# Routing in ten even pieces, four softmax rows on VectorE from step 48, and the shared expert of two groups inside attention's last steps

## The chip, the cores and the metric

The kernel runs on one core of a Trainium2 chip. Its time is the device time of one execution in microseconds (us). PE is TensorE (matrix products; PEld its weight loads), DVE is VectorE, ACT is ScalarE, POOL is GpSimd, SP is SyncE, which issues most transfers (DMA). Each engine works through its own list of instructions in order; one that waits for a semaphore holds back everything behind it on that engine.

## What is computed

The input is 4096 tokens (16 sequences of 256) of 128 numbers, in float32. Two layers follow each other; in each, `x = x + attention(norm(x)) + ffn(norm(x))`. The change touches layer 0 alone:

```python
xn = layernorm(x)
# attention: 8 heads of 64, windows of 128 (a block of 256 queries sees 256 keys under a mask)
qkv = (layernorm(xn) * ln_g + ln_b) @ w_qkv.T       # q and k rotated by position
out = softmax(mask(q @ k.T)) @ v @ w_out.T
# ffn: 8 routed experts, two for each token, and one shared expert
probs = softmax(xn @ router_w + router_b); two largest -> weights
shared = gelu(xn @ sw1 + sb1) @ sw2 + sb2
routed = sum over the two experts of weight * (gelu(xn @ rw1[e] + rb1[e]) @ rw2[e] + rb2[e])
x = x + out + shared + routed
```

Layer 1 (a gated attention unit and 32 experts) comes after it and has the same code in both kernels but for one helper that is called in other pieces.

## The kernel before

**Tiling.** Tokens go in 8 groups of 512 (`G`), a group being 4 chunks of 128 tokens, and two sequences. Layer 0's attention is a loop of 64 steps (line 531, s from -3 to 64): one step is one sequence and one pair of heads, eight steps are a group (`g, r = divmod(s, 8)`). The loop is software-pipelined and its order is written by hand: inside `tc.manual_schedule` (line 497) every engine gets its instructions in the order of the program text. What one turn of the loop at step s issues, in this order:

- copies left from the turn before (`later`): on ACT, the values `v` out of PSUM (line 363) and `here`, a copy of the q/k projection (387), whose halves four DMAs on SP exchange into `there`;
- on PE, the 8 transposes of the weights of step s (`turned0`, 456); on ACT, their eviction to `pT` (463), and then the 4 exponentials of step s+2 (433), each with its row sum;
- on DVE, every second step `near` (q and k times cosine, 394, two of 512 columns);
- on DVE, `divided` for step s+1 (439 to 442): a reciprocal and **three of the four** row blocks times it. The fourth is done by ACT (`divided_last`, 447), later in the same turn, behind the exponentials;
- on DVE, on the other steps, `far` ("there" times sine, 398);
- `scores` for step s+3: 4 matmuls on PE (417; the profile counts each fp32 matmul twice) and 4 reductions on DVE (423) that add the mask, move the scores out of PSUM and take the row maximum;
- `sums` (402): cosine part plus sine part, on POOL for pairs of heads 1 to 23 (`FREE = 24`, line 370), on DVE for 0 and 24 to 31;
- then one piece of the routing, of the preparing or of the placing, if the tables of due times say so (below);
- ACT's fourth row block (447); on PE the product with the values of step s-1 (`attended`, 473), on ACT its copy (478);
- on odd steps the next q/k projection (`rotated`, 377), on r = 0 and 2 a half of the output projection (`project`, 486), on r = 4 and 6 two of the four value projections (362).

**Side work in the loop.** For each group `routed` (334) makes norms, transposes the normalised tokens, and calls `route0` (214): router matmuls (219), logits and maximum (222 to 225), exponential (228), and then in one piece sum, reciprocal, probabilities and `before` (197), which ranks the 8 probabilities of a token by 8x8 comparisons in five operations (203 to 212). The dictionary `pieces` (512) gives group g = 1 to 7 a first step of -6, -1, 4, 10, 15, 21, 26 and its pieces 0, 2, 5, 6, 7, 8 and 9 steps later. `prepare` (349) makes the second normalisation, and its first piece (`xh`, 173) is due at r = 6, two groups ahead. `places0` (239) counts tokens for each expert in eight pieces, from step 37; its results `slot_at` and `tile_off` say in which row of `x_rows` (in HBM) a token goes. From step 43 each turn issues three scatters on POOL (316, 64 in all), each behind one ACT instruction of the same turn.

**After the loop** (686) the shared expert of groups 0 and 1 (`shared0`, 608: two matmuls with `sw1`, two Gelus, two matmuls with `sw2`, an add into `yTs`) and the routed experts (706): 39 tiles of 256 rows, each fetched (643 weights, 645 rows) by SP, transposed, multiplied, and stored. Here a scheduler orders the instructions. The buffers of this stage lie where attention's were, so that the first fetch waits for the last use of them. The other six groups' shared expert is done in layer 1's beginning (934 to 940).

PSUM has 8 banks: two for scores (`s`), two for transposes (`t`), one for `o`, three for all else (`mm`); `turn` (61, 602) says from which tags `mm_tile` takes its banks.

Of the kernel before, what the change touches and what calls it, by code (L numbers as in the profile page):

```python
# [47 lines left out]
def two_layers(ctx: ExitStack, tc: tile.TileContext, a: dict, out: bass.AP):  # L48
# [17 lines left out]
    def mm_tile(name):  # L66
        tags, n = turn
        turn[1] += 1
        return bank(tags[n % len(tags)], name)
# [125 lines left out]
        return d  # L195

    def before(rank, v, tie, n, name):

        v_o = v.unsqueeze(2).to_broadcast([P, NC, n, n])
        v_i = v.unsqueeze(3).to_broadcast([P, NC, n, n])  # L200
        gt = small.tile([P, NC, n, n], F32, tag=f"gt{n}", name=f"gt_{name}", bufs=2)
        eq = small.tile([P, NC, n, n], F32, tag=f"eq{n}", name=f"eq_{name}", bufs=2)
        nc.vector.tensor_tensor(gt, v_o, v_i, ALU.is_gt)
        nc.vector.tensor_tensor(eq, v_o, v_i, ALU.is_equal)
        nc.vector.tensor_tensor(
            eq.rearrange("p c i j -> p c (i j)"),
            eq.rearrange("p c i j -> p c (i j)"),
            tie.unsqueeze(1).to_broadcast([P, NC, n * n]),
            ALU.mult,
        )  # L210
        nc.vector.tensor_tensor(gt, gt, eq, ALU.add)
        nc.vector.tensor_reduce(rank, gt, AX.X, ALU.add)

    def route0(g, xnT):

        ps_r = mm_tile(f"rt_{g}")
        ps_r = ps_r[:, : NC * E0].rearrange("p (c e) -> p c e", e=E0)
        for c in range(NC):
            nc.tensor.matmul(ps_r[:, c, :], xnT[:, c * P : (c + 1) * P], rtw, start=True, stop=True)
        yield  # L220
        lg = small.tile([P, NC, E0], F32, tag="lg", name=f"lg_{g}")
        nc.vector.tensor_tensor(lg, ps_r, rtb, ALU.add)
        mx = small.tile([P, NC], F32, tag="rmx", name=f"rmx_{g}")
        nc.vector.tensor_reduce(mx, lg, AX.X, ALU.max)
        nc.vector.tensor_tensor(lg, lg, mx.unsqueeze(2).to_broadcast([P, NC, E0]), ALU.subtract)
        yield
        pr = pr_all[:, g * NC : (g + 1) * NC, :]
        nc.scalar.activation(pr, lg, AF.Exp)
        yield
        sm = small.tile([P, NC], F32, tag="rsm", name=f"rsm_{g}")  # L230
        nc.vector.tensor_reduce(sm, pr, AX.X, ALU.add)
        nc.vector.reciprocal(sm, sm)
        nc.vector.tensor_tensor(pr, pr, sm.unsqueeze(2).to_broadcast([P, NC, E0]), ALU.mult)
        before(rk_all[:, g * NC : (g + 1) * NC, :], pr, tie0, E0, f"r0_{g}")
        yield

    scattered = []
# [75 lines left out]
    def scatter0(n, behind):  # L313
# [12 lines left out]
        )  # L326
        scattered.append(ins)


    yTs, xnTs = [], []  # L330
    with first as pa:
        wk = pa.enter_context(tc.tile_pool(name="wkA", bufs=2))

        def routed(g):
            xn = xn_all[:, g * NC : (g + 1) * NC, :]
            stats = moments(xs[g], f"a{g}")
            yield
            again(r2_all[:, g, :], *normalise(xn, xs[g], *stats), f"b{g}")
            yield
            t = transposed(xn, f"xnT_{g}")  # L340
            xnT = keep.tile([P, G], F32, tag="xnT", name=f"xnTs_{g}")
            nc.scalar.copy(xnT, t)
            xnTs.append(xnT)
            yield
            yield from route0(g, xnT)
# [21 lines left out]

        paces = [None] * 3
        later, turning = [], []
        FREE = 24  # L370

        def rotated(n):

# [63 lines left out]

        def divided(s, pr, sm):
            nc.vector.reciprocal(sm, sm)
            for n in range(3):  # L440
                row = pr[:, n // 2, n % 2, :]
                nc.vector.tensor_scalar(row, row, sm[:, n : n + 1], None, ALU.mult)  # L442

# [53 lines left out]
        with tc.manual_schedule(engines={order.PE, order.DVE, order.Activation, order.Pool}):  # L497
# [11 lines left out]
                fs.clear()  # L509


            pieces = {}
            for g, begin in zip(range(1, NG), (-6, -1, 4, 10, 15, 21, 26)):
                for d in (0, 2, 5, 6, 7, 8, 9, 10):
                    pieces.setdefault(begin + d, []).append(g)

            step(routing, 0, 2)
            step(preparing, 0, 2)
            rotated(0)
            drain(later)  # L520
# [1 line left out]
            near, far, sums = turning.pop(0)  # L522
            near()
            step(routing, 0)
            step(routing, 1, 2)
            far()
            sums()
            drain(later)
# [2 lines left out]
            for s in range(-3, NS + 1):  # L531
                g, r = divmod(s, 8)
                if 0 <= s < NS:
                    tps = turned0(s, sc.pop(s)[0])
                drain(later)
                if 0 <= s < NS:
                    pTs[s] = evicted(s, tps)
                if 0 <= s + 2 < NS:
                    sms[s + 2] = exponentials(s + 2, *sc[s + 2])
                if turning and len(turning[0]) == 3:  # L540
                    turning[0].pop(0)()
                    far = sums = None
                else:
                    far, sums = turning.pop(0) if turning else (None, None)
                if 0 <= s + 1 < NS:
                    sm = sms.pop(s + 1)
                    divided(s + 1, sc[s + 1][0], sm)
                if far:
                    far()
                if s + 3 < NS:  # L550
                    sc[s + 3] = scores(s + 3)
                if sums:
                    sums()

                if s in (-3, -2, -1, 5):
                    step(routing, 0)
                if s == -2:
                    step(preparing, 1)
                for n in pieces.get(s, ()):
                    step(routing, n)  # L560
                if r == 0:
                    step(preparing, g + 1)
                if s >= 0 and r == 6:
                    step(preparing, g + 2)
                if s == 37:
                    placing = places0(wk)
                if 37 <= s < 45:
                    next(placing)
                if 0 <= s + 1 < NS:
                    divided_last(sc[s + 1][0], sm)  # L570
                if s >= 1:
                    attended(s - 1, pTs.pop(s - 1))

                if s % 2 and 2 <= (s + 7) // 2 < NS // 2:
                    rotated((s + 7) // 2)
                if s < -1:
                    for c in range(2):
                        values(0, 2 * (s + 3) + c)
                if s < 0:
                    continue  # L580
                if 0 < g < NG and r in (0, 2):
                    project(g - 1, r // 2)
                if s == NS - 2:
                    project(NG - 1, 0)
                if r in (4, 6) and g + 1 < NG:
                    values(g + 1, r - 4)
                    values(g + 1, r - 3)
                if s == 2:
                    zero = w_a.tile([P, 2 * D], F32, tag="zero", name="zero")
                    nc.gpsimd.memset(zero, 0.0)  # L590
                    x_r0 = x_rows.rearrange("(t p c) d -> p t (c d)", p=P, c=2)

                if s >= 2 and s % 2 == 0 and s - 2 < NT0:
                    n = min(2, NT0 - (s - 2))
                    nc.sync.dma_start(
                        out=x_r0[:, s - 2 : s - 2 + n, :], in_=zero.unsqueeze(1).to_broadcast([P, n, 2 * D])
                    )
                if s >= 43:
                    for n in range(3 * (s - 43), min(3 * (s - 42), 2 * NG * NC)):
                        scatter0(n, paces[n % 3])  # L600
            project(NG - 1, 1)
    turn[0] = ["mm", "s", "mm", "o", "mm", "s"]


    late = ctx.enter_context(tc.tile_pool(name="late", bufs=1))
    spread = ctx.enter_context(tc.tile_pool(name="spread", bufs=4))

    def shared0(g, wk):
        hs = []
        for c in range(2):  # L610
            hp = mm_tile(f"hs_{g}_{c}")
            nc.tensor.matmul(hp, sw1[:, c * P : (c + 1) * P], xnTs[g], start=True, stop=True)  # L612
            h = wk.tile([P, G], F32, tag="h1", name=f"hss_{g}_{c}", bufs=6)
            nc.scalar.activation(h, hp, AF.Gelu, bias=col("sb1", c))
            hs.append(h)
        yield
        yp = acc_tile(f"y1_{g}")
        for c, h in enumerate(hs):
            nc.tensor.matmul(yp, sw2[:, c, :], h, start=(c == 0), stop=(c == 1))
        nc.vector.tensor_tensor(yTs[g], yTs[g], yp, ALU.add)  # L620
        yield

    with ExitStack() as pb:
        wk = pb.enter_context(tc.tile_pool(name="wkB", bufs=2))
# [58 lines left out]
            nc.vector.tensor_tensor(y, yp, bias, ALU.add)  # L683
            nc.sync.dma_start(out=yr[t], in_=y)

        for g in range(2):
            for _ in shared0(g, wk):
                pass
        stage = [fetched, turned, hidden, down]
        at = [0, 4, 5, 6]  # L690
        state = {}
# [31 lines left out]
    with ExitStack() as pc:  # L723
# [207 lines left out]
        begun = {n: pair(0, n) for n in range(-1, 3)}  # L931
        with tc.manual_schedule(engines={order.PE, order.DVE, order.Activation, order.Pool}):

            shared = {f"y{g}": shared0(g, wk) for g in range(2, NG)}
            steps1 = {"n": finish0(0), "r": choice, "a": attention, "f": coming,
                      **{f"p{n}": b for n, b in begun.items()}, **shared}
            for what in (
# [136 lines left out]
```

## Time and profile before

| what | us |
| --- | --- |
| median of 3 runs | 962.4 |
| lowest, highest | 961.96, 965.62 |
| the profiled execution itself | 969.97 |
| its span, from which all times below are counted | 968.2 |
| first exponential of step 0 starts | 33.83 |
| of step 48; of step 58; last exponential of the loop ends | 277.25; 329.53; 358.8 |
| last matmul of attention ends, first fetch of the routed experts is issued | 372.0; 372.12 |
| PE, DVE, ACT, POOL busy, of the span | 94%, 73%, 51%, 30% |

How to read it: busy shares over the whole span mix stages with different limits, so the views used below are cut at the times in the table. A profile line of a group has its source line, engine, operation, tiles and count, then busy time, mean duration in ns of one, and the idle time just before them with the engine and line that ended it. The chain of waits is followed back from the last instruction, each step to what released it. The granted clock is the share of PE's full clock in a stretch.

### The profile page before, as it was taken

How to read it: one execution, taken by the hardware profiler on the slowest of the kernel's cores; microseconds unless marked ns; L12 is line 12 of the kernel's file. 1: busy time of each engine (PE TensorE's matmuls, PEld its weight loads, DVE VectorE, ACT ScalarE, POOL GpSimd, SP SyncE). 2: the span in 40 equal slices, each digit the busy share in tenths (PEclk: the TensorE clock that was granted, in tenths of full speed). 3: DMA queues.
4: the chain of work that ended last, by engine and by line, in shares of the span. 5: the costliest groups of instructions: out<-in, count | busy, mean ns of one | idle time of the engine just before them, and what ended most of it. 6: DMA issues, size and time to landing. Idle time of an engine off the chain costs nothing.

```text
span 968.2 us, 13569 instructions
## 1 busy us (share of the span) xinstructions
PE 909.4 (94%) x3848; PEld 516.2 (53%) x3848; DVE 705.3 (73%) x2247; ACT 498.6 (51%) x1216; POOL 286.1 (30%) x253
## 2 busy tenths in 40 slices
PE   2998999999999888998989999999999999999997
PEld 1555566565555444988445445454455545455453
DVE  4699999889999741333379588686876868778663
ACT  1688889889787873433352233433324342243411
POOL 2242343332355562000353124241242512321200
PEclk8799999999999999999999999999999999999999
DMA  6061111011122115787135432323333243321430
GB/s 194 23 218 45 28 24 33 24 27 29 28 69 64 58 39 188 223 256 222 42 77 131 103 77 70 99 76 98 77 97 91 63 93 96 92 77 44 101 87 11
DMA packets 64921, 84.54 MB, mean 87 GB/s; under 512 B 10320, under 2 KB 40784, under 8 KB 64336
## 3 DMA queue, kind: packets, MB, share of 16 engines
q1 hardware_dynamic: 60320, 74.75, 28.8%
q0 software_dynamic: 4096, 8.40, 2.8%
q8 instruction: 31, 0.51, 0.2%
q10 hardware_dynamic: 432, 0.53, 0.2%
q14 instruction: 42, 0.34, 0.1%
HBM read 58.22 MB, written 17.04 MB: 78 GB/s over the span
## 4 chain that ended last, share of the span: by engine, by line
PE 59%; DVE 23%; issue 6%; DMA 5%; ACT 3%; POOL 2%; SPq 2%; DVEq 0%; ACTq 0%; POOLq 0%
PE u L919 9%; PE g L917 7%; PE z L954 7%; PE s L417 5%; PE o L473 3%; DVE p L423 3%; PE y L486 3%; PE t L456 3%; PE h L665 3%; PE yr L676 3%; DVE p L442 2%; DMA y_rows<-yt 2%; PE z L972 2%; PE o L892 1%; PE pq L377 1%
## 5 line engine op out<-in xcount | busy, mean ns | idle before, releaser
L921 ACT ACTIVATE h<-g 128x512 f32<-128x512 f32 x128 | 75.2, 594 | 234.5 <-PE g L917 222.3
L923 DVE TENSOR_TENSOR h<-h,u 128x512 f32<-128x512 f32 x128 | 87.3, 683 | 63.8 <-PE u L919 57.0
L917 PE MATMUL g<-xn1Ts,eg 128*128 128x512 f32 x256 | 131.4, 595 | 0.0
L919 PE MATMUL u<-xn1Ts,eu 128*128 128x512 f32 x256 | 131.2, 597 | 0.0
L433 ACT ACTIVATE p<-p,nm 128x256 f32<-128x256 f32 x256 | 127.6, 515 | 0.3
L954 PE MATMUL z<-h,ed 128*128 128x512 f32 x224 | 114.2, 593 | 0.0
L423 DVE CUSTOM_DVE_ANT_0 p<-s,mask 128x256 f32<-128x256 f32 x256 | 92.9, 419 | 16.0 <-PE s L417 15.2
L732 POOL DMA_INDIRECT yg<-y_rows,slot_at x64 | 69.7, 1090 | 114.4 <-PE hs L612 96.1
L417 PE MATMUL s<-k,q 64*128 64x256 f32 x512 | 85.2, 420 | 12.2 <-DVE k L402 7.6
L926 DVE TENSOR_TENSOR h<-h,bc 128x512 f32<-128x512 f32 x128 | 90.3, 708 | 2.7
L456 PEld LDWEIGHTS t<-ident,p 128*128 128x128 f32 x512 | 59.1, 140 | 51.1 <-ACT p L447 13.2
L456 PE MATMUL t<-ident,p 128*128 128x128 f32 x512 | 69.4, 275 | 14.0 <-ACT p L447 9.0
L316 POOL DMA_INDIRECT x_rows<-xn_all,slot_at x64 | 63.7, 996 | 52.0 <-ACT pT L463 15.2
L463 ACT COPY pT<-t 128x512 f32<-128x512 f32 x128 | 69.5, 598 | 18.4 <-PE t L456 13.9
L919 PEld LDWEIGHTS u<-xn1Ts,eu 128*128 128x128 f32 x256 | 48.1, 193 | 54.4 <-issue 47.8
L954 PEld LDWEIGHTS z<-h,ed 128*128 128x128 f32 x224 | 42.5, 190 | 53.3 <-issue 46.5
L917 PEld LDWEIGHTS g<-xn1Ts,eg 128*128 128x128 f32 x256 | 46.3, 190 | 46.0 <-issue 41.4
L473 PE MATMUL o<-pT,v 128*64 128x256 f32 x512 | 70.7, 398 | 0.0
L402 POOL TENSOR_TENSOR q<-q,sq 128x512 f32<-128x512 f32 x23 | 36.2, 1576 | 115.2 <-DVE sq L398 96.2
L863 POOL TENSOR_TENSOR r1s<-r1s,sinr 128x512 f32<-128x512 f32 x16 | 23.6, 1480 | 157.2 <-ACT r1s L858 153.6
L417 PEld LDWEIGHTS s<-k,q 64*128 64x128 f32 x512 | 50.8, 193 | 33.1 <-DVE nm L423 10.0
L668 ACT ACTIVATE h0s<-h,we 128x256 f32<-128x256 f32 x78 | 32.7, 470 | 53.0 <-issue 35.5
(252 smaller groups left out, 1581.2 us busy)
## 6 DMA issues: line engine op xcount, KB each, us to landing
bc<-rows_r SPq DMA_DIRECT2D x128, 256.0 KB
there<-here SPq DMA_DIRECT2D x128, 64.0 KB
we<-in_ex_dram SPq DMA_DIRECT2D x39, 129.0 KB
xt<-x_rows SPq DMA_DIRECT2D x39, 128.0 KB
y_rows<-yt SPq DMA_DIRECT2D x39, 128.0 KB
x_rows<-zero SPq DMA_DIRECT2D x19, 256.0 KB
x<-in_x_dram SPq DMA_DIRECT2D x8, 256.0 KB
out_dram<-out SPq DMA_DIRECT2D x8, 256.0 KB
```

The costliest lines, as they stand in the source:

```text
L417: nc.tensor.matmul(sp[h][:, i, :], q[rows, b, i * P : (i + 1) * P], k[rows, b, :], start=True, stop=True)
L423: nc.vector.tensor_tensor_reduce(out=pr[:, h, i, :], in0=sp[h][:, i, :], in1=mask[:, i, :], scale=-1.0, scalar=-NEG, op0=ALU.add, op1=ALU. ...
L433: paces[1] = nc.scalar.activation(row, row, AF.Exp, bias=nm[:, n : n + 1], scale=-1.0, accum_out=sm[:, n : n + 1])
L456: nc.tensor.transpose(tp[:, at : at + P], pr[:, h, i, j * P : (j + 1) * P], ident)
L473: nc.tensor.matmul(op[h * DH : (h + 1) * DH, :], vs[g][:, 2 * b + j, (2 * hp + h) * DH : (2 * hp + h + 1) * DH], pT[:, h, j, :], start=(j ...
L732: nc.gpsimd.indirect_dma_start(out=yg[:, 2 * c + s, :], out_offset=None, in_=y_rows, in_offset=bass.IndirectOffsetOnAxis(ap=slot_at[:, s, ...
L917: nc.tensor.matmul(gp, wg, xn1Ts[g], start=True, stop=True)
L919: nc.tensor.matmul(up, wu, xn1Ts[g], start=True, stop=True)
L921: nc.scalar.activation(h, gp, AF.Silu)
L923: nc.vector.tensor_tensor(h, h, up, ALU.mult)
L926: nc.vector.tensor_tensor(h, h, spread_w[g][n // 2][:, n % 2, :], ALU.mult)
L954: nc.tensor.matmul(zp, w, r, start=(n == 1), stop=False)
```

## The change

Nothing is computed differently; the same instructions are moved, but for 16 row blocks that go from ACT to DVE and one pair of additions that goes from POOL to DVE.

1. `before` yields twice, after the first comparison and after the tie product, and `routed` yields between `normalise` and `again`: a group's routing has ten pieces instead of seven. A new table gives their steps (first step 5g-12), with own rows for groups 0, 1 and 7; `xh` gets a table too (`turned_rows`).
2. In a turn of the loop, the pieces of routing, preparing and placing move up: behind `divided`, ahead of `far`, `scores` and `sums`.
3. `SHARED = 48`: for steps 48 to 63 all four row blocks are divided on DVE, and ACT's instruction falls away.
4. `FREE` is 23: the sums of pair 23 go to DVE.
5. Placing starts at step 35, scattering at step 41 (two earlier each).
6. `shared0` is cut in four pieces, and groups 0 and 1 run inside the loop's last turns, in buffers of attention's pool (tags `here`, `there`), with `mm_tile` alternating between the tags `mm` and `s`. Their last two pieces come behind `project(NG - 1, 1)`.

In the built order of the new kernel, SP's first DMA behind the loop (`uvu`, a weight of layer 1) waits for the last matmul of group 1's shared expert, and `tile_off` is read and the first rows and weights are fetched behind it; in the kernel before, SP had read `tile_off` ahead of its wait, and waited for the last matmul of `project`.

```diff
     def before(rank, v, tie, n, name):
+        for _ in before_in_parts(rank, v, tie, n, name):
+            pass
+
+    def before_in_parts(rank, v, tie, n, name):
...
         nc.vector.tensor_tensor(gt, v_o, v_i, ALU.is_gt)
+        yield
         nc.vector.tensor_tensor(eq, v_o, v_i, ALU.is_equal)
...
+        yield
         nc.vector.tensor_tensor(gt, gt, eq, ALU.add)
         nc.vector.tensor_reduce(rank, gt, AX.X, ALU.add)
...
-        before(rk_all[:, g * NC : (g + 1) * NC, :], pr, tie0, E0, f"r0_{g}")
+        yield from before_in_parts(rk_all[:, g * NC : (g + 1) * NC, :], pr, tie0, E0, f"r0_{g}")
...
+    def shared0(g, wk, tags=("h1", "h1"), bufs=6):
+        hs = []
+        for c in range(2):
+            hp = mm_tile(f"hs_{g}_{c}")
+            nc.tensor.matmul(hp, sw1[:, c * P : (c + 1) * P], xnTs[g], start=True, stop=True)
+            h = wk.tile([P, G], F32, tag=tags[c], name=f"hss_{g}_{c}", bufs=bufs)
+            hs.append((h, hp))
+            if c == 0:
+                yield
+        yield
+        for c, (h, hp) in enumerate(hs):
+            nc.scalar.activation(h, hp, AF.Gelu, bias=col("sb1", c))
+        yield
+        yp = acc_tile(f"y1_{g}")
+        for c, (h, _) in enumerate(hs):
+            nc.tensor.matmul(yp, sw2[:, c, :], h, start=(c == 0), stop=(c == 1))
+        nc.vector.tensor_tensor(yTs[g], yTs[g], yp, ALU.add)
+        yield
...
-            again(r2_all[:, g, :], *normalise(xn, xs[g], *stats), f"b{g}")
+            at = normalise(xn, xs[g], *stats)
+            yield
+            again(r2_all[:, g, :], *at, f"b{g}")
...
-        FREE = 24
+        SHARED = 48
+        FREE = 23
...
-            for n in range(3):
+            for n in range(3 if s < SHARED else 4):
...
-            for g, begin in zip(range(1, NG), (-6, -1, 4, 10, 15, 21, 26)):
-                for d in (0, 2, 5, 6, 7, 8, 9, 10):
-                    pieces.setdefault(begin + d, []).append(g)
+            for g in range(NG):
+                b = 5 * g - 12
+                ranks = (b + 12, b + 13, b + 14)
+                if g == 0:
+                    at = (-3, -2, -1, 0, 1, 2)
+                elif g == 1:
+                    at = (-1, 0, 1, 2, 4, 5, 6)
+                elif g == NG - 1:
+                    at = (b, b + 1, b + 2, b + 3, b + 4, b + 5, b + 6, b + 9, b + 10, b + 11)
+                else:
+                    at = (b, b + 1, b + 2, b + 4, b + 6, b + 8, b + 9, *ranks)
+                for n in at:
+                    pieces.setdefault(n, []).append(g)
+            turned_rows = {2: 7, 3: 12, 4: 22, 5: 27, 6: 37, 7: 47}
...
                     divided(s + 1, sc[s + 1][0], sm)
+
+                if s == -2:
+                    step(preparing, 1)
+                for n in pieces.get(s, ()):
+                    step(routing, n)
+                if r == 0:
+                    step(preparing, g + 1)
+                for n in turned_rows:
+                    if turned_rows[n] == s:
+                        step(preparing, n)
+                if s == 35:
+                    placing = places0(wk)
+                if 35 <= s < 43:
+                    next(placing)
                 if far:
                     far()
...
-                if s in (-3, -2, -1, 5):
-                    step(routing, 0)
...
-                if s >= 0 and r == 6:
-                    step(preparing, g + 2)
-                if s == 37:
...
-                if 0 <= s + 1 < NS:
+                if 0 <= s + 1 < SHARED:
                     divided_last(sc[s + 1][0], sm)
...
-                if s >= 43:
-                    for n in range(3 * (s - 43), min(3 * (s - 42), 2 * NG * NC)):
+                if s >= 41:
+                    for n in range(3 * (s - 41), min(3 * (s - 40), 2 * NG * NC)):
                         scatter0(n, paces[n % 3])
+
+                if s == NS - 3:
+                    turn[0] = ["mm", "s", "mm", "s", "mm"]
+                    shared = [shared0(g, wk, ("here", "there"), 2) for g in range(2)]
+                    next(shared[0])
+                elif s == NS - 2:
+                    next(shared[0])
+                elif s == NS - 1:
+                    next(shared[0])
+                    next(shared[1])
+            next(shared[1])
+            next(shared[0])
             project(NG - 1, 1)
+            next(shared[1])
+            next(shared[1])
...
-        for g in range(2):
-            for _ in shared0(g, wk):
-                pass
...
-            shared = {f"y{g}": shared0(g, wk) for g in range(2, NG)}
+            shared = {f"y{g}": joined(shared0(g, wk), 3, 1) for g in range(2, NG)}
```

`joined` runs the first three pieces of `shared0` as one and the last as another, so that layer 1's hand-written order has two pieces for a group as before. The old `shared0` had the Gelu of each half right behind its matmul, and two pieces.

More of the change, by code (lines that the diff above doesn't have):

```diff
@@ L327, in scatter0, with joined @@
         scattered.append(ins)
+    def joined(gen, *parts):
+        for n in parts:
+            for _ in range(n):
+                next(gen)
+            yield
[17 more added lines that the diff above has]
+        yield
     yTs, xnTs = [], []
@@ L337, in routed @@
             yield
-            again(r2_all[:, g, :], *normalise(xn, xs[g], *stats), f"b{g}")
+            at = normalise(xn, xs[g], *stats)
+            yield
+            again(r2_all[:, g, :], *at, f"b{g}")
             yield
@@ L512, in two_layers @@
             pieces = {}
-            for g, begin in zip(range(1, NG), (-6, -1, 4, 10, 15, 21, 26)):
-                for d in (0, 2, 5, 6, 7, 8, 9, 10):
-                    pieces.setdefault(begin + d, []).append(g)
-            step(routing, 0, 2)
+            for g in range(NG):
[12 more added lines that the diff above has]
+            turned_rows = {2: 7, 3: 12, 4: 22, 5: 27, 6: 37, 7: 47}
+            step(routing, 0, 3)
             step(preparing, 0, 2)
@@ L524, in two_layers @@
             step(routing, 0)
-            step(routing, 1, 2)
+            step(routing, 1, 3)
             far()
@@ L553, in two_layers @@
                     sums()
-                if s in (-3, -2, -1, 5):
-                    step(routing, 0)
[L557 to L562, printed above, removed]
-                if s >= 0 and r == 6:
-                    step(preparing, g + 2)
-                if s == 37:
-                    placing = places0(wk)
-                if 37 <= s < 45:
-                    next(placing)
-                if 0 <= s + 1 < NS:
+                if 0 <= s + 1 < SHARED:
                     divided_last(sc[s + 1][0], sm)
@@ L606, in two_layers @@
     spread = ctx.enter_context(tc.tile_pool(name="spread", bufs=4))
[L608 to L621, printed above, removed]
     with ExitStack() as pb:
```

## The prediction

> **What bounds the kernel now.** The change touches the time from 31 us to about 384 us (routed experts running). I first cut that into stages by the times in the table above and asked for the busy time of each engine. Columns: stage, its length, then PE (instructions), PEld, DVE, ACT and POOL busy, granted clock, DMA share, GB/s.
>
> ```profile
> 36.04:277.25 241.21, 230.08 (x1361) 136.30 (x1359) 228.74 (x906) 208.37 (x637) 82.97 (x66) 1.00 0.18 50
> 277.25:329.53 52.28, 47.62 (x280) 27.81 (x282) 46.15 (x164) 43.66 (x134) 29.90 (x31) 0.99 0.22 64
> 329.53:358.73 29.20, 24.42 (x141) 13.46 (x137) 16.78 (x69) 21.37 (x71) 16.29 (x17) 0.90 0.15 47
> 358.73:372.12 13.39, 11.00 (x46) 5.15 (x47) 1.29 (x4) 4.42 (x13) 8.74 (x9) 0.91 0.14 47
> ```
>
> DVE is busy for 228.74 of 241.21 us up to step 48: it is the bound there (PE, 230.08, is as full by the page, but its ends are modelled). From 277 on DVE has slack, and from 329 much; something else ends the waits. So I read the waits of DVE from 277.25 to 372.12 next (engine, line, releaser: us in total, times, longest):
>
> ```profile
> DVE p L423 <- PE s L417: 7.1, 5, 2.9
> DVE sm L439 <- ACT p L433: 5.8, 2, 4.8
> DVE q L394 <- ACT here L387: 4.3, 3, 1.5
> ```
>
> and then the chain of waits there (start, length, what):
>
> ```profile
> 335.19 1.07 ACT pT L463 x2
> 336.26 1.97 ACT p L433 x8
> 338.23 0.41 ACT p L447
> 338.64 0.05 issue
> 338.68 0.55 PE t L456 x3
> 339.23 1.06 PE s L417 x8
> 340.29 1.01 PE o L473 x8
> 341.31 1.91 PE y L486 x4
> 343.22 0.87 PE t L456 x8
> ...
> 369.61 2.38 PE y L486 x2
> ...
> 372.12 0.38 SPq L643
> ```
>
> The reader is to see a serial loop of two steps: ACT must finish four exponentials (1.97) before its own fourth row block (L447), PE's transposes wait for that block, and PE then works through all of a step while ACT waits in turn. PE's transposes wait 8.3 us for L447 after 277. The last line is the fetch of the routed experts, released by attention's last matmul.
>
> One more view, of 3.41 us: the granted clock is halved there, and twice more, at 328.73 and 369.69 (0.51 each).
>
> ```profile
> 349.21:352.62 3.41, 3.41 (x16) 1.95 (x16) 1.64 (x9) 3.23 (x11) 2.50 (x4) 0.51 0.11 38
> ```
>
> **The change, part by part** (negative is gain).
>
> A, *head of the loop*. From 30.84 to 35.31 DVE is idle (4.47, waiting for PE's scores of step 1). Afterwards it makes logits of group 0 (36.69 to 37.24, 0.55), `xh` of group 1 (0.78 to the next start) and, at 41.60, the moments of group 2 (1.26). The built order now has all of these ahead of the reductions of step 1, in that idle time. From 36 on DVE is full, so -2.6. Ends: -2.6, and 0 if PE, still half-clocked there, is delayed by as much.
>
> B, *even pieces ahead of the scores, to step 48*. DVE's work is the same; what can go is its idle time, 241.21 - 228.74 = 12.5 us, of which 7.0 are named waits (3.6 for scores L417, 3.4 for `here` L387) and the rest small gaps at each semaphore. The waits come behind lumps: a whole ranking is some 3 us (0.18 + 0.18 + 0.70, then five of about 0.42), ahead of the next division, and PE waits for that division. New pieces that fall in a step with first step b modulo 5 are 1.4, 1.1, 1.7, 1.4 and 0.8 us, and they come behind the division. Against it: PE's own pieces (router 6.3/6 = 1.05, two transpositions 3.9/6 = 0.65 each, a group) now stand in front of the scores that DVE waits for. Ends: -7.0 (all named waits) and +3.9 (0.65 new, six groups). I take -5, nearer the first, because DVE has 1 us more per step of its own in front of those scores. The longer-held PSUM bank of the logits adds waits of value projections for `near` (10 instead of 6 in the built order), which precedes them by a step's work; cost 0, up to the 1.2 of one `near` each if that cover goes, inside the +3.9.
>
> C, *`FREE`*: two additions on DVE, 0.69 + 0.68 in row L402, at step 41 where DVE is full: +1.4; 0 at the other end. POOL loses 1.59 + 1.27, which nothing waited for. Placing and scatters two steps earlier: the same instructions; the last scatter in the profile ends at 370.3, below the fetch, so 0 either way.
>
> D, *fourth row on DVE, steps 48 to 57* (277.25 to 329.53). +10 x 0.35 (L442) on DVE: 46.15 + 3.5 = 49.7 of 52.28. DVE's waits for `here` (4.3) follow ACT's exponentials and L447, and ACT loses 10 x 0.41. I take -1 (51.3: 1.6 of idle stay). Ends: -2.6 (no idle stays) and +3.5 (all of it stays).
>
> E, *fourth row, steps 58 to 63* (329.53 to 358.73). With L447 gone from the chain, t waits for DVE's rows, which follow the exponentials by 0.17 + 4 x 0.35 = 1.6 while PE has a step of work. I add up PE from the end of its transposes of step 56 to those of step 61, by rows of the chain: t 0.87, s 1.06, o 1.01, y 1.91. 5 s (5.3) + 5 o (5.05) + 5 t (4.35) + 2 y (3.8) = 18.5. Then pT 1.07 and the last exponentials 1.97: 329.53 + 21.5 = 351.1. DVE's own sum for steps 56 and 57, with four rows, is 9.2 (pitch 0.60 for six of 512 columns, 0.345 for eight reductions, 0.3 for eight rows, 0.2 for two reciprocals); from 328.72 that ends at 337.9, where it ends now at 338.7, so it doesn't hold PE back. Ideal -7.6; I take -6.5, leaving 1.1 for latencies. Ends: -7.6 and 0.
>
> F, *the drain*, from the last exponentials (now 358.73) to the fetch (372.12): 13.4 now. New: by the built order PE has, behind those exponentials, o(61) at +0.4 (it waits for ACT's copy of o(60)), y 1.9, a shared `sw1` matmul 0.95 (L619 and L612 go at 0.46 an instruction, two each), t(63) to +5.2, o(62), `sw1` to +7.1, o(63) to +8.1, `sw1` to +9.05. ACT meanwhile: copy, table load 1.28, two Gelus 1.2, copy of o(63) at +9.5. PE: group 0's `sw2` to +10.95, last half of `project` to +12.85. Then ACT: yT 0.7, two Gelus of group 1, and PE's last two `sw2`: +16.2. SP's first DMA waits for that last matmul. So +2.8; with a half-clocked window like the present one 1.7 more. I take +3.5; ends +1.2 (Gelus of group 1 hidden) and +4.6.
>
> G, *start of the routed experts*. Now the fetch starts at 372.12 and PE waits for rows until 382.98; `sw2` and two `sw1` (until 378.5) lie in that gap. Taking them out saves nothing there: the gap is DMA. SP now reads `tile_off` behind its wait (L633, 524 to 993 ns): +0.6, and +0.3 for a PE idle for some 5 us. Ends +0.5 and +2.3.
>
> A rule that speaks against the change: while PE was busy 24.42 of 29.20, the clock was halved in windows of 3.41. The Trainium skill, "TensorE: Matmul & The Clock Gate", section "What's actually happening", says that an idle window of about 3.4 us halves the clock until a busy one. The empty gap of G would then start cold: by the page the sum would be 1.7 worse, by the rows 0.3. Another: the table load takes 1.28 and Gelu starts 0.02 after it. "ScalarE: Activation LUTs", "What ACT_TABLE_LOAD costs", adds 1.38 of drain to it; the row has none, so by the page F would be +4.9, by the row +3.5.
>
> **Sum**: -2.6 - 5 + 1.4 - 1 - 6.5 + 3.5 + 0.9 = **-9.3 us**. The profiled execution is 969.97, the median 962.4: 7.6 us that I cannot place and take to stay. 969.97 - 9.3 = 960.7 in a profile, **953.1** in the median.
>
> **Rivals.**
>
> *Given back* (960): the loop's gain is real in the tail alone. B and A give nothing (PE's pieces ahead of the scores cost what the lumps cost), C, D to G as above: 1.4 - 1 - 6.5 + 3.5 + 0.9 = -1.7, about 960.7. For it: PE's 230.08 of 241.21. Against: the five DVE waits sit behind lumps.
>
> *DVE becomes the bound of the tail* (slower): DVE has the fourth rows, the sums of pair 23 to 31 and `near`, and if each wait for `here` stays (its ACT copy stands behind four exponentials of 1.97 whatever becomes of L447), the rows are pure cost: A -2.6, B 0, C 1.4, D +3.5, E 0, F and G 4.4: +6.7, 969. It decides when DVE's rows of a step come later than PE finishes the step before them, that is when DVE, not PE, is the later one from 329.53 on. For it: 49.7 of 52.28. Against: the slack of 12.4 us in the next stage.
>
> *Twice as even* (946): all named waits go, the tail runs without idle and the clock stays full: -2.6 - 7 + 1.4 - 2.6 - 7.6 + 1.2 + 0.9 = -16.3.
>
> That the change doesn't do what it says can be ruled out for the order, which is built; but the scheduler had already two of the four `sw1` matmuls inside attention (357.09 and 364.57), so the shared expert moves by less than its name.
>
> **Chances.** Forecast (948 to 957) 0.52, given back (957 to 965) 0.20, slower 0.15, twice as even 0.13. The range leaves out the far end of the slower case and some of the best: 946 to 967. About 0.5% (4.8 us) is what a measurement of this kernel can tell from no change: faster 0.65, same 0.20, slower 0.15.
>
> **What would show it.** A: no wait over 2 us of DVE before 36. B: named waits of DVE to step 48 under 3. E: no ACT row L447 behind step 47, few t waits, pairs of steps after 329 of 8 us instead of 10. F: the first DMA behind attention released by a `sw2` matmul, some 16 us after the last exponential. G: about 11 us from it to steady tiles. It is wrong if DVE's busy time from step 48 on comes within a few per cent of that stage, or if the drain is over 19.

## The result and the profile after

The changed kernel takes **947.6 us** (median; 944.2 to 948.6), the kernel before beside it 962.2: 0.984 of it, 95% interval 0.980 to 0.987, a gain of 14.6. The later runs come from three more sets, each on one chip; the kernel before took 972.2, 961.9 and 974.6 there, so every kernel is set against the kernels of its own set. The changed kernel took 962.3 in the second set (0.989 of the kernel before; 0.985 to 0.992) and 950.7 in the third (0.989; 0.988 to 0.991): gains of 10.0 and 11.1. The forecast was 953.1, a gain of 9.3, most likely between 948 and 957: the first result lies 0.4 below that, and the two later gains, of about its size, fit it.

The profiled execution of the changed kernel took 944.23, its span 942.5. The stages are cut as before: loop up to the exponentials of step 48, to step 58, to the last exponential, to SP's first DMA behind the loop, to the first matmul of the routed experts' third tile (from where tiles follow each other without a gap). Columns as in the first view: stage, length, then busy time of PE, PEld, DVE, ACT and POOL, granted clock, DMA share, GB/s.

```profile
31.17:268.16 236.99, 230.49 (x1374) 140.19 (x1372) 225.70 (x909) 210.13 (x645) 87.82 (x70) 0.99 0.19 52
268.16:313.12 44.96, 44.96 (x276) 26.65 (x275) 44.60 (x163) 40.20 (x125) 31.48 (x31) 1.00 0.26 75
313.12:335.29 22.17, 21.98 (x144) 13.05 (x140) 18.89 (x77) 18.86 (x66) 15.49 (x16) 1.00 0.19 57
335.29:351.41 16.12, 14.51 (x56) 6.25 (x54) 2.27 (x7) 7.81 (x16) 3.94 (x5) 1.00 0.06 21
351.41:364.08 12.67, 5.71 (x22) 3.89 (x22) 2.34 (x5) 1.68 (x4) 0.00 (x0) 0.87 0.81 259
```

The reader is to see three things. From step 48 to 58 DVE is now busy for all of the stage (44.60 of 44.96), as PE is by its modelled ends, and the stage is shorter than before (52.28). The next stage is no longer a serial loop (22.17, with PE at 21.98, after 29.20 with PE at 24.42). And the drain is longer than before (16.12 after 13.4).

DVE's waits up to step 48 (engine, line, releaser: us in total, times, longest), the first by `here`, the second by PE's scores:

```profile
DVE q L429 <- ACT here L422: 4.6, 6, 1.3
DVE p L458 <- PE s L452: 1.6, 1, 1.6
```

PE's waits for ACT's fourth row from step 0 to the last exponential, before (L447) and after (L482, which exists up to step 47 only):

```profile
PE t L456 <- ACT p L447: 7.9, 7, 1.9
```

```profile
PE t L491 <- ACT p L482: 1.4, 2, 0.9
```

And the chain of waits around the drain (start, length, what):

```profile
349.35 2.00 PE y L357 x4
...
351.37 0.70 DVE yT L358
...
352.07 0.49 SPq L678
...
356.14 6.93 DMA xt<-x_rows
```

The drain ends as forecast: with group 1's `sw2` products (L357), then the read of `tile_off` (L678) on SP, then the rows.

All profiles of this study, in the same stages (us); the last tile is counted up to the end of its first products (`h`):

| kernel | start of step 0 | 0 to 48 | 48 to 58 | 58 to last exponential | to the third tile | to the last tile | rest |
| --- | --- | --- | --- | --- | --- | --- | --- |
| before | 33.8 | 243.4 | 52.3 | 29.2 | 25.2 | 77.2 | 507.0 |
| changed | 31.2 | 237.0 | 45.0 | 22.2 | 28.8 | 74.6 | 503.8 |
| e0_again | 31.4 | 237.1 | 49.7 | 22.6 | 34.2 | 79.8 | 505.5 |
| e1_share64 | 30.4 | 236.6 | 51.5 | 28.4 | 30.9 | 76.0 | 505.3 |
| e2_old_routing | 34.1 | 244.7 | 52.0 | 24.5 | 31.2 | 81.3 | 505.3 |
| e3_shared_behind | 31.4 | 237.1 | 50.8 | 24.4 | 25.8 | 81.3 | 506.1 |
| f0_again | 31.0 | 237.0 | 45.0 | 22.2 | 28.6 | 78.2 | 504.5 |
| f1_kept | 31.7 | 235.4 | 45.0 | 22.2 | 25.7 | 79.0 | 504.9 |
| f2_behind_sums | 33.0 | 250.0 | 44.9 | 22.2 | 28.8 | 77.6 | 503.8 |
| f3_share_only | 33.1 | 242.4 | 47.5 | 22.3 | 25.5 | 82.2 | 504.0 |
| g0_before | 34.5 | 246.4 | 53.3 | 30.1 | 25.9 | 82.6 | 505.8 |
| g1_share64 | 31.2 | 237.3 | 52.4 | 29.7 | 30.7 | 78.5 | 505.9 |
| g2_shared_behind | 31.1 | 235.7 | 52.3 | 30.7 | 25.4 | 80.0 | 505.7 |
| g3_lumps_ahead | 32.4 | 245.1 | 50.3 | 29.2 | 32.1 | 82.1 | 505.8 |

Between the first two rows every stage differs, by 25.7 in all, though the times differ by 14.6: the profile before is 7.8 above the median of 962.2, the profile after 3.3 below its own. A difference of two profiles is thus not yet a cause, and the experiments had to say which of it belongs to the change.

### The profile page after: what moved, and what is told of

Read it like the earlier page. It is cut to its first block, busy times and chain, and to the rows that moved or that the text cites. A ratio compares the mean times of both kernels' runs of the same rounds, so it can differ in the third digit from the quotient of the medians.

```text
span 942.5 us, 13590 instructions
## 1 busy us (share of the span) xinstructions
PE 898.5 (95%) x3848; PEld 515.2 (55%) x3848; DVE 703.2 (75%) x2265; ACT 491.7 (52%) x1200; POOL 286.8 (30%) x251
## 4 chain that ended last, share of the span: by engine, by line
PE 52%; DVE 6%; DMA 2%; issue 1%; SPq 1%; ACT 0%; POOL 0%; DVEq 0%
PE u L961 11%; PE g L959 10%; PE z L996 9%; PE yr L721 3%; PE h L710 3%; PE o L934 3%; PE z L1014 2%; PE pv L883 1%; PE s L919 1%; PE pu L889 1%; PE y L357 1%; DVE h L968 1%; PE hs L346 1%; DMA y_rows<-yt 1%; PE xn1T L179 1%
## 5 line engine op out<-in xcount | busy, mean ns | idle before, releaser
L774 POOL DMA_INDIRECT yg<-y_rows,slot_at x64 | 69.8, 1090 | 121.6 <-PE hs L346 103.4
L491 PEld LDWEIGHTS t<-ident,p 128*128 128x128 f32 x512 | 59.5, 140 | 35.1 <-issue 8.6
L322 POOL DMA_INDIRECT x_rows<-xn_all,slot_at x64 | 66.0, 1032 | 38.1 <-ACT pT L498 16.0
L491 PE MATMUL t<-ident,p 128*128 128x128 f32 x512 | 67.3, 273 | 1.4 <-ACT p L482 1.4
L477 DVE TENSOR_SCALAR p<-p,sm 128x256 f32<-128x256 f32 x208 | 62.0, 356 | 2.3
```

Source lines behind the costliest of these rows:

```text
L491: nc.tensor.transpose(tp[:, at : at + P], pr[:, h, i, j * P : (j + 1) * P], ident)
L774: nc.gpsimd.indirect_dma_start(out=yg[:, 2 * c + s, :], out_offset=None, in_=y_rows, in_offset=bass.IndirectOffsetOnAxis(ap=slot_at[:, s, ...
```

## The experiments

The theory after the first result: the terms add up, with sizes as the two profiles show them (routing 9 to 12, rows 11 to 14, shared expert +3.6). The rivals are named with each run.

**e0_again**: no edit.

> The changed kernel once more, unaltered, as the base of the three beside it: 944 to 949 us (its four runs gave 944.2 to 948.6). If the halved-clock windows are what makes the profiled executions differ (six of them in the profile before, four after), the windows will lie at other times in this profile while the time from the first to the last exponential of the loop stays within 3 us of 304.

Measured 962.3; from the first to the last exponential 309.4 in place of 304. So the bound of 3 us was missed: the loop to step 48 repeats to 0.1 us here (between 235.4 and 237.3 in all eight profiles of kernels that are as changed up to step 48), steps 48 to 58 don't (49.7 against 45.0, at full clock). More on that in the last section.

**e1_share64**: the rows undone.

```diff
-        SHARED = 48
+        SHARED = 64
```

> ScalarE divides the fourth row in all steps again (D and E undone), all else as changed. Theory (the rows on VectorE are worth what the two profiles show between steps 48 and 63, 11 to 14 us, since the chain exponentials, fourth row, transposes was serial): 958 to 962. Rival 1 (the prediction's size, 1 + 6.5): 955. Rival 2 (the difference of the two profiles there is three halved-clock windows of the profile before, at most 1.7 each, and the rows are worth little): 948 to 952.

Measured 967.9 where the changed kernel took 962.3: **+5.7**, 0.9955 of the kernel before (0.993 to 0.998). Between the rivals' sizes; neither the 11 to 14 of the profiles nor nothing. The size is uncertain: the changed kernel's own interval is 0.985 to 0.992.

**e2_old_routing**: pieces, table and place of routing, preparing and placing, and the scatters' step, as in the kernel before; the diff is the reverse of points 1, 2 and 5 of the change.

> Routing, preparing and placing again in the old pieces, at the old steps and behind the sums, scatters from step 43 (A and B undone; C to G stay). Theory (worth what the profiles show to step 48, 9 to 12 with C's 1.4 in it): 957 to 960. Rival 1 (the prediction's 7.6): 955. Rival 2 (given back: even pieces gain nothing in a loop that PE fills): 946 to 950.

Measured 974.2: **+11.9** over the changed kernel. It is what the theory said of the two profiles, and more than the 7.6 forecast. Against e0_again's profile, 2.7 of it lie ahead of step 0 and 7.6 between 0 and 48.

**e3_shared_behind**: the shared expert of groups 0 and 1 behind the loop.

```diff
-                if s == NS - 3:
...
-            next(shared[1])
-            next(shared[0])
             project(NG - 1, 1)
-            next(shared[1])
-            next(shared[1])
...
+        for g in range(2):
+            for _ in shared0(g, wk):
+                pass
         stage = [fetched, turned, hidden, down]
```

> The shared expert of groups 0 and 1 behind the loop again, ahead of the routed experts (F and G undone; A to E stay). Theory (it only lengthened the drain, +3.5, and left an empty gap in front of the first tile, +0.9): 943 to 944, and the first fetch some 13.4 us behind the last exponential in place of 16.1. Rival (the old place costs as much, because its matmuls stand in front of the first tile): 947 to 948.

Measured 954.5, **7.8 below** the changed kernel of its set and 0.981 of the kernel before (0.978 to 0.985); the time from the last exponential to the third tile is 25.8 in place of 34.2. More than either theory. But that 34.2 is e0_again's; the same stretch took 28.8 and 28.6 in the two other profiles of the changed kernel. In e0_again the clock is halved inside it from 343.37 to 350.20, ahead of the first fetch, and in neither of the others there.

**f0_again**: no edit.

> The changed kernel once more, as the base of the three beside it. On the chip of the first four experiments it took 962.3, 0.989 of the kernel before; in its own four runs 947.6, 0.984. Expected 0.984 to 0.990 of the kernel before.

Measured 950.7, 0.989 (0.988 to 0.991).

**f1_kept**: the wait on group 1's products alone.

```diff
-                    shared = [shared0(g, wk, ("here", "there"), 2) for g in range(2)]
+                    shared = [shared0(0, wk, ("here", "there"), 2), shared0(1, keep, ("hsa", "hsb"), 1)]
```

> As changed, but the two Gelu results of group 1's shared expert lie in buffers that live on, so that SP's first DMA behind the loop waits for the last matmul of project and not for the last sw2 matmul of group 1. Nothing else in the order moves. Theory (the wait on those products is what F costs; project's last matmul ends 3.3 us ahead of them in both profiles of the changed kernel): the first fetch 3.3 us earlier, the time 3 to 4 us below the changed kernel's. Rival (the cost is the six shared matmuls that stand in front of project on PE, and the halved clock around them): no more than 1 us below.

Measured 947.7, **3.0 below** f0_again; the 95% intervals against the kernel before (0.985 to 0.988, and 0.988 to 0.991) hardly overlap. SP's first DMA in f0_again and in f1_kept:

```profile
351.24 0.35 SPq L76 DMA_DIRECT2D uvu<-in_uvu_dram  x1
```

```profile
347.02 0.35 SPq L76 DMA_DIRECT2D uvu<-in_uvu_dram  x1
```

The last exponentials end at 335.1 and 334.2, so the DMA comes 3.3 us sooner behind them (16.1, then 12.8), as the theory said. So the wait on the products is a cost of its own, and larger than the rival allowed. That the products which stand in front of `project` cost nothing is not shown.

**f2_behind_sums**: the new pieces and table in the old place.

```diff
                     divided(s + 1, sc[s + 1][0], sm)
-                if s == -2:
...
-                    next(placing)
                 if far:
...
                 if sums:
                     sums()
+                if s == -2:
...
+                    next(placing)
```

> As changed, with the ten even pieces and the new table, but the pieces stand where they stood before, behind the sums instead of ahead of far and scores. Undoing pieces, table and place together cost 11.9. Theory 1 (evenness is what counts): 0 to 4 above the changed kernel, 2.7 of it the head of the loop. Theory 2 (the place counts: behind the sums a piece stands in front of the next division, for which PE's transposes wait): 7 to 12 above.

Measured 963.6, **+12.8** over f0_again and 1.003 of the kernel before (1.000 to 1.006): the even pieces in the old place are no better than the lumps there. Theory 2's size, but not its mechanism. The equality test of the ranking, the first operation of an even piece, in f2_behind_sums (mean 1117 ns) and in f0_again (418):

```profile
L209 DVE TENSOR_TENSOR eq_r<-pr_all 128x256 f32<-128x256 f32 x8 | 8.9, 1117 | 0.0
```

```profile
L209 DVE TENSOR_TENSOR eq_r<-pr_all 128x256 f32<-128x256 f32 x8 | 3.3, 418 | 0.0
```

One of the eight in f2_behind_sums, by its timeline, with what POOL does at that time:

```profile
103.21 1.27 POOL L437 TENSOR_TENSOR k<-k,sk 128x512 f32<-128x512 f32 x1
...
103.42 1.35 DVE L209 TENSOR_TENSOR eq_r<-pr_all 128x256 f32<-128x256 f32 x1
```

DVE's operation of 0.42 starts while POOL adds k (`sums`, until 104.48) and ends just behind it, at 104.77. It is counted as busy all the time, so that no view of waits shows it. In the kernel before the same:

```profile
142.60 1.27 POOL L402 TENSOR_TENSOR k<-k,sk 128x512 f32<-128x512 f32 x1
...
143.22 0.70 DVE L233 TENSOR_TENSOR pr_all<-pr_all,rsm 128x32 f32<-128x32 f32 x1
```

and by groups, L233 before and the same instruction, L239, after:

```profile
L233 DVE TENSOR_TENSOR pr_all<-pr_all,rsm 128x32 f32<-128x32 f32 x8 | 3.7, 460 | 0.3
```

```profile
L239 DVE TENSOR_TENSOR pr_all<-pr_all,rsm 128x32 f32<-128x32 f32 x8 | 1.5, 191 | 0.3
```

I summed, between steps 0 and 48, all DVE operations that take over 0.3 us more than the shortest execution of the same operation in any profile here: nine of them, 5.6 us, in the kernel before; 16, 13.7 us, in f2_behind_sums; none in the changed kernel. Each of them overlaps POOL's addition of k. f2_behind_sums takes 250.0 there and f0_again 237.0, and DVE's busy time (the third engine in these rows) is 14.5 more:

```profile
33.00:283.00 250.00, 239.86 (x1374) 141.68 (x1372) 240.27 (x919) 211.35 (x646) 86.46 (x70) 0.98 0.18 49
```

```profile
31.03:268.00 236.97, 230.45 (x1374) 140.27 (x1372) 225.78 (x909) 209.97 (x646) 87.82 (x70) 0.99 0.19 53
```

So the 13.0 are, in the main, these 13.7.

**f3_share_only**: the kernel before with the fourth row on DVE from step 48 (`SHARED = 48`, the loop over four rows, the bound of `divided_last`), nothing else.

> The kernel before with the fourth row on VectorE from step 48 and nothing else (D and E alone). If the parts add up: 5.7 us below the kernel before (what undoing them in the changed kernel cost). By the prediction's terms: 7.5 below. Rival (it only works with the routing moved, since VectorE has the sums of pairs 24 to 31 there): no change.

Measured 961.2 beside 961.9: 0.9998 (0.998 to 1.002). **No gain**, though its profile has 69.8 us from step 48 to the last exponential where the profile before has 81.5. The rival's number came, but not its reason: DVE does the rows with the old routing as well. The two stages of the loop behind step 48 and the stretch to the third tile, in f3_share_only:

```profile
275.52:323.03 47.51, 47.13 (x280) 27.71 (x282) 47.16 (x171) 40.41 (x125) 31.01 (x31) 1.00 0.24 70
323.03:345.31 22.28, 22.10 (x144) 13.09 (x140) 19.01 (x77) 18.89 (x66) 15.68 (x16) 1.00 0.19 57
345.31:370.80 25.49, 18.90 (x78) 9.32 (x77) 4.62 (x11) 9.57 (x19) 9.77 (x11) 0.97 0.49 160
```

It is nearly as quick there as the changed kernel (47.5 and 22.3, against 45.0 and 22.2). So the 81.5 of the profile before is no measure of what the rows save.

**g0_before**: the kernel before, no edit.

> The kernel before, unaltered, for a second profile. Its first profiled execution took 969.97 where its runs lie at 961 to 966. Theory (that execution was held up between steps 48 and 63, where products that PE had finished were waited for by ScalarE for some us more): steps 48 to the last exponential take 73 to 77 us instead of 81.5, and the rows' worth of the two first profiles, 14.4, shrinks to 6 to 10 (the changed kernel takes 67.1 there). Rival (that stretch is as long in every execution, and the 8 us lie behind it): 80 to 82.

Inconclusive: 975.0, and its profiled execution, at 83.4 from step 48 to the last exponential, is again one of the long ones (span 978.6). The rival's 80 to 82 is nearer, but it is hard to square with the set where f3_share_only, at 69.8, gained nothing. The kernel before has no profile in that set.

**g1_share64**: as e1_share64, in the fourth set.

> Once more the changed kernel with ScalarE's division in all steps, since undoing the rows cost 5.7 there, and adding them alone to the kernel before gained 0.7 (up to 2.2). Base: the changed kernel at 0.989 of the kernel before. Theory 1 (the rows gain only where the drain behind them is the changed one): 4 to 7 above the base, 0.994 of the kernel before. Theory 2 (they gain next to nothing, and the first result was the disturbed stretch): within 2 of the base, 0.989 to 0.991.

Measured 967.5, 0.993 of the kernel before (0.990 to 0.995). The changed kernel had 0.989 in two sets, and didn't run in this one; at that rate, an assumption here and in the two runs below, the rows' undoing costs 3.6. Between the two theories.

**g2_shared_behind**: as e3_shared_behind, in the fourth set.

> Once more the changed kernel with the shared expert of groups 0 and 1 behind the loop, 7.8 below the changed kernel at first. Of that the wait on group 1's last products is 3.0 (measured by itself). Theory 1 (the rest is the shared matmuls in front of project, and is there in every execution): 7 to 9 below the base, 0.980 to 0.982 of the kernel before. Theory 2 (the rest was held-up products in the base's drain): 3 to 5 below, 0.984 to 0.986.

Measured 963.5, 0.988 (0.984 to 0.992): at 0.989 for the changed kernel, next to no gain. The stretch it is meant to shorten is short (25.4), but steps 58 to the last exponential took 30.7 in its profile, where that kernel's first profile has 24.4. Neither theory.

**g3_lumps_ahead**: the old seven pieces and steps in the new place (the reverse of point 1 of the change but for the table of `xh`, with point 2 left as it is).

> As changed, with routing in the seven old pieces at the old steps (a whole ranking in one piece), but in the new place, ahead of far and scores. The even pieces in the old place took 12.8 more than the changed kernel, as much as old pieces in the old place. Theory 1 (the place is all, and a lump of 3 us does no harm there): 0 to 3 above the base. Theory 2 (a lump ahead of the scores holds PE up, so that both are needed): 5 to 12 above.

Measured 972.3, 0.9985 (0.996 to 1.001): some 8 above the changed kernel at 0.989. Theory 2. Up to step 48 no DVE operation is held by POOL here (none over 0.3 us), but the waits are these:

```profile
PE s L450 <- DVE nm L456: 8.3, 11, 1.5
DVE q L427 <- ACT here L420: 7.7, 11, 1.3
DVE p L456 <- PE s L450: 5.0, 5, 2.6
```

A lump of 3 us ahead of the reductions makes PE wait for a free bank of scores (8.3 after 2.6 in f0_again), and DVE then for the scores (5.0 after 1.5) and for `here` (7.7 after 4.5).

## Why the prediction was right in sum and wrong in two terms

**A, right in size.** DVE has no wait over 1.1 us between 20 and 36, and step 0 starts 2.7 sooner (33.8 to 31.2; 2.7 between e2_old_routing and e0_again), where -2.6 was forecast. Part of it can be the clock: the half-clocked start ends at 35.1 in the profile before and at 28.6 in the one after. In f3_share_only, with the old order there, PE is at full speed by 31.4 (two value projections take 1.13 us, 2.08 at that place in the profile before) and step 0 starts at 33.1; in f1_kept, with the new order, the half clock ends at 30.1 and step 0 starts at 31.7. So some 1.4 is left where the clock differs little. Why the half clock ends sooner is not shown.

**B, the step that failed by size and by reason.** "DVE's work is the same; what can go is its idle time" set the far end at -7.0. B and C together shortened steps 0 to 48 by 6.4 between the first two profiles, by 5.4 between f3_share_only and f0_again, and by 9.1 and 10.7 in the fourth set (g0_before, with two halved windows in that stretch, against g1_share64 and g2_shared_behind), where -3.6 was forecast; in time, undoing A and B cost 11.9 against 7.6. Most of it isn't idle time. DVE's busy time fell from 229.4 in f3_share_only, whose order up to step 48 is the old one, to the 225.8 of f0_again shown above:

```profile
33.08:275.52 242.44, 231.34 (x1368) 136.97 (x1364) 229.38 (x908) 210.24 (x646) 83.02 (x66) 1.00 0.18 49
```

It fell although C added 1.4, because nine operations no longer run into POOL's addition (5.6). The named waits, in f3_share_only these, fell only from 9.7 to 6.0, not to under 3:

```profile
DVE p L424 <- PE s L418: 6.3, 5, 2.6
DVE q L395 <- ACT here L388: 3.4, 4, 1.9
```

Those for scores went (6.3 to 1.5), those for `here` grew (3.4 to 4.5). The two experiments with one half of B each show that either half alone gains nothing clear of the noise (1.003 and 0.9985 of the kernel before, where e2_old_routing, with neither, has 1.0016): the place takes the operations off POOL's back, and only even pieces can stand there without holding up the scores. The Trainium skill, "SBUF — State Buffer", section "SBUF: two separate sides", says that DVE and GpSimd share a pair of ports, and that an operation of either that needs it holds it as an exclusive lock for its whole length while the other blocks; on DVE's side it names those with two SBUF inputs, against a GpSimd operation that reads SBUF, and those in a 2-port mode. These traces agree: held by POOL's addition, for up to 0.95 us, were tensor_tensor from SBUF, tensor_scalar and copy; not held beside the same addition were `near` (one input in PSUM, 0.68 either way), the reductions of scores, reciprocals and batch statistics. The prediction didn't weigh that rule, and had one of the nine in its own working: the 0.70 of the lump ("0.18 + 0.18 + 0.70") is L233 blocked, which takes 0.19 when it is free.

**C** was not measured by itself.

**D and E, oversized.** By the profiles -7.3 and -7.0 against -1 and -6.5, so they seemed right or too small. By the times the rows gain 0.7 alone (at most 2.2), clearly less than the 7.5 forecast, and cost 5.7, perhaps 3.6, when undone, which the intervals don't tell from 7.5. Whether, and why, they are worth more in the changed kernel than alone stays open. The failing step is the one ahead of the sum: "7.6 us that I cannot place and take to stay". The stages from 277 to 359, from which D and E were priced, are the ones that repeat badly between executions; a long one there was taken for the usual one. That the missing 7.6 lay there is argued, not shown, since both profiles of the kernel before are long ones. What the forecast said of the order came true: no fourth row on ACT behind step 47, PE's waits for it 1.4 in place of 7.9, and two steps in 8.1 to 8.9 behind 58 where the forecast had 8 and before 10.

D's -1 was moreover wrong in its own working: the 46.15 of DVE in that window held work for 43 reductions and six pairs, ten steps need 40 and five. Cut by ACT's instructions, a window holds whatever DVE happens to be ahead.

**The rival "DVE becomes the bound"** was half right: DVE is full from 48 to 58 (44.60 of 44.96), as PE is by its modelled ends. The forecast took that for a sign of loss. It was none here: the stage got shorter.

**F and G, right.** In the profile +2.7 and +0.8, against +3.5 and +0.9. The wait on the `sw2` products, named as F's cause, is worth 3.0 to 3.3 by itself. In time the whole of F and G cost 7.8 once and next to nothing the other time; only the 3.0 is safe.

The sum came out near partly by luck: B was too small, and D and E, by what they gain alone, too large. In the second set the parts undone one at a time add up (11.9 + 5.7 - 7.8 = 9.8 of the 10.0 gained there); the rows alone in the third set (0.7) and the shared expert in the fourth (next to nothing) don't fit that sum.

## What to carry to other kernels

Look at the longest, not the mean, of an operation that runs many times on DVE: where its long executions end just behind a POOL instruction, as here, it was held up, counts as busy, and is gained back by moving it. When a profiled execution is slower than the median, find where it is slower, with a second profile, before a stage of it is priced. And let work be last in a stage if it must, but not in buffers that the next stage's first transfer needs.

A version that beats both kernels is f1_kept (947.7 beside 950.7 and 961.9); e3_shared_behind did so by more once and not the second time.

## What the runs showed that was not expected

**Products that are waited for after they are done.** From step 48 on, while the scatters run, some executions hold ACT up. In e0_again PE's four products into `o` end at 269.89 (the trace models the ends of products), and ACT, free from 270.96, copies them at 272.74:

```profile
268.81 1.08 PE L508 MATMUL o<-pT,v 128*64 128x256 f32 x8
...
270.44 0.52 ACT L482 ACTIVATE p<-p,sm 128x256 f32<-128x256 f32 x1
...
272.74 0.37 ACT L513 COPY oT<-o 128x256 f32<-128x256 f32 x1 [1.78 <-PE t L491]
```

In the first profile of the changed kernel the same copy follows at once:

```profile
268.50 1.08 PE L508 MATMUL o<-pT,v 128*64 128x256 f32 x8
...
270.14 0.52 ACT L482 ACTIVATE p<-p,sm 128x256 f32<-128x256 f32 x1
270.54 0.38 ACT L513 COPY oT<-o 128x256 f32<-128x256 f32 x1
```

In e0_again the trace has no signal of PE's semaphore from 268.9 to 272.7, and then five within 0.2 us. Gaps of 1.4 us and more that end like this, with three signals or more within 0.2 us, come between steps 48 and 63 in both profiles of the kernel before and in all of the second and fourth set; in the changed kernel's first profile and in the third set there is none. They go with the two sets in which the kernel before is 10 to 13 us longer. What holds the signals back stays open.

**Where a halved window falls decides its price.** Around the first tiles the clock is halved in every profile, for 3.41 or 6.83 us; in the first of the kernel before alone the window begins ahead of the first fetch. In f0_again that is 355.96 to 362.79, ahead of the third tile, and the next six tiles take 12.2 us. In f3_share_only it is 369.06 to 375.89, and they take 14.6; in f1_kept, 357.78 to 364.61, 14.4, which took 2.2 of what the earlier fetch had gained by then. The Trainium skill's rule on the idle window ("TensorE: Matmul & The Clock Gate", "What's actually happening"), weighed in the prediction, fits the halved windows behind an empty PE of 4.2 to 4.8 us, as in f0_again (4.48). In f1_kept and f3_share_only PE's longest gap there, by its modelled ends, is 1.9 and 2.0 us, shorter than the rule's 3.4, and the clock was halved all the same. The 1.7 worked out from the rule is neither floor nor ceiling: the cost was 0 in f0_again and 2.2 and 2.4 in the other two.
